# Perceiver block on one core: loads of the first stage on one queue, the first K summed chunk by chunk, first queries turned between the quarters of V

## The chip, the cores and the metric

The kernel runs on one core of a Trainium2 chip. The metric is the device time of one execution in microseconds (us), from the runs of the kernel; beside it there is the profile of one execution. A core has a matrix engine (PE, with its weight loads shown as PEld), a vector engine (DVE), a scalar engine (ACT), GpSimd (POOL) and a sync engine (SP) that only issues transfers. ACT and POOL can issue transfers too. On-chip memory holds the tiles (128 partitions); PE writes into eight accumulation banks, from which ACT or DVE copy.

## What is computed

Thirty-two batches of 64 tokens, 512 features each, attend to 512 context rows of 384 features (16 heads of 32); then the tokens attend to each other, causally and with rotary positions; then half of the tokens of each batch, chosen by a router score, go through a feed-forward layer. All in float32. The first of the three blocks is the one that matters here:

```python
def _L0_xattn_ref(x, context, context_mask, Wq, Wk, Wv, Wo):
    q = (x @ Wq).reshape(B, N, HEADS, hd).transpose(0, 2, 1, 3)
    k = (context @ Wk).reshape(B, M, HEADS, hd).transpose(0, 2, 1, 3)
    v = (context @ Wv).reshape(B, M, HEADS, hd).transpose(0, 2, 1, 3)
    scores = jnp.einsum('bhid,bhjd->bhij', q, k) * scale
    scores = jnp.where(context_mask[:, None, None, :], scores, max_neg)
    attn = jax.nn.softmax(scores, axis=-1)
    out = jnp.einsum('bhij,bhjd->bhid', attn, v)
    return out.transpose(0, 2, 1, 3).reshape(B, N, DIM) @ Wo

x = x + _L0_xattn_ref(_layernorm(x), ctx_768, mask, Wq, Wk, Wv, Wo)
x = x + _L0_attn_ref(_layernorm(x), wq, wk, wv, wo)
x = x + _L0_ffn_ref(_layernorm(x), w_router, W1, b1, W2, b2)
```

## The kernel before

The 2048 token rows are sixteen tiles of 128 rows (`xs[t]`, two batches each); four tiles are a query group (`GT = 4`, eight batches). Every stage is unrolled in Python. A float32 product of 128x128 by 128x512 is two PE instructions, so K of one batch (four pieces of 128 columns, each a sum over three chunks of the context's 384 features) is 24 instructions, and V likewise.

**First stage.** The constants (identity for the transposes, the exponent -0.5, masks) and all sixteen tiles of x are loaded from ACT's queue (lines 74 and 80). The weights of the cross attention, `wk`, `wv`, `wq`, `wo`, are loaded from POOL's queue (164 to 168, through `load`, line 70), each in one transfer; the context of a batch (768 KB, transposed on the host) and its mask come from SP's queue (`load_ctx`, 157). Then, at line 351 and on, PE does K of batch 0 piece by piece (`kv_piece`, 181: three chunks summed into one bank, then a copy, by ACT for K, by DVE for V), V of batch 0, the turns of the first four normalised tiles, and the first group's queries (`query_chunk`, 215). A turn (`query_turn`, 211) is four transposes on PE into bank "pt" and one copy by ACT; `query_norm` (205) writes its rows into a tile `xn` of which there is one. So norm, transposes and copy of one tile alternate. The statistics of a tile (`ln_stats`, 86) are two instructions on DVE and two on POOL. In this stage only PE's order is the written one (`manual_schedule(engines={PE})`); for the other engines a planner orders the instructions.

**Banks.** `bank` (61) names them: "mm" has two, "pt", "po" and "sc0" to "sc3" one each. A product into a bank that is still being copied waits for the copy.

**Loop over batches** (`step`, two steps a batch, all engines in the written order). A step makes the scores of eight heads into sc0 to sc3 (`score_burst`), the softmax on DVE, ACT and POOL into tiles `pr` (a ring of eight), splits and turns the probabilities by transfers on SP's queue (`part`, line 281), joins them one step later (`join`), and uses them two steps later (`attend`). Between them PE works on the next batch's K (first step) or V (second step), and in the first four batches of a group on the next group's turns. At the first step of batch b SP issues the context of batch b + 2.

After the loop come the self attention (lines 509 to 671) and the feed-forward, in which PE's order is written out and the planner orders the rest.

Of the kernel before, what the change touches and what calls it, by code (L numbers as in the profile page):

```python
# [7 lines left out]
F32 = mybir.dt.float32  # L8
U8 = mybir.dt.uint8
# [6 lines left out]
P = 128  # L16
NB, S, D = 32, 64, 512
M, DC = 512, 384
# [4 lines left out]
NC = D // P  # L23
# [19 lines left out]
def perceiver_block(  # L43
# [17 lines left out]
    def bank(tag, shape, name):  # L61
        return psum.tile(shape, F32, tag=tag, name=name, bufs=2 if tag == "mm" else 1)
# [4 lines left out]
    def load(pool, w, tag, name, engine):  # L67
        k, f = w.shape
        t = pool.tile([P, w.shape[0] // P if tag == "W2" else NC, f], F32, tag=tag, name=name)
        engine.dma_start(t[:, : k // P, :], chunked(w))  # L70
        return t

    cst = const.tile([P, C_END], F32, tag="cst", name="cst")
    nc.scalar.dma_start(cst, consts)
    ident = cst[:, C_ID : C_ID + P]

    xs = []
    for t in range(NT):
        xt = xpool.tile([P, D], F32, tag=f"x{t}", name=f"x{t}")
        nc.scalar.dma_start(xt, x[t * P : (t + 1) * P, :])  # L80
        xs.append(xt)

    mv = [const.tile([P, NT, 2], F32, tag=f"mv{n}", name=f"mv{n}") for n in range(3)]
    rstd = [const.tile([P, NT], F32, tag=f"rstd{n}", name=f"rstd{n}") for n in range(3)]
# [11 lines left out]
    def ln_apply(dst, n, t):  # L96
        nc.vector.tensor_scalar(
            dst, xs[t], mv[n][:, t, 0:1], rstd[n][:, t : t + 1], ALU.subtract, ALU.mult
        )

    def transposed(tag, src, name):

        ps = bank(tag, [P, NC, P], f"{name}_tp")
        for c in range(NC):
            nc.tensor.transpose(ps[:, c, :], src[:, c * P : (c + 1) * P], ident)  # L105
        return ps
# [45 lines left out]
    with ExitStack() as pa:  # L152
# [4 lines left out]
        def load_ctx(b):  # L157
            t = kvp.tile([P, NCC, M], F32, tag="ctxT", name=f"ctxT{b}")
            nc.sync.dma_start(t, chunked(ctxT[b]))
            m8 = kvp.tile([P, M], U8, tag="m8", name=f"m8_{b}")  # L160
            nc.sync.dma_start(m8, mask[b : b + 1, :].to_broadcast([P, M]))
            return t, m8

        wk = load(wbpool, xWk, "wk", "xWk", nc.gpsimd)
        ctx0 = load_ctx(0)
        wv = load(wbpool, xWv, "wv", "xWv", nc.gpsimd)
        wq = load(wbpool, xWq, "wq", "xWq", nc.gpsimd)
        wo = load(wbpool, xWo, "wo", "xWo", nc.gpsimd)

        def kv_start(b, loaded):  # L170
            cT, m8 = loaded
            v = kvp.tile([P, NKC, D], F32, tag="v", name=f"v{b}")
            return dict(b=b, cT=cT, m8=m8, kT=[None] * NC, v=v)
# [31 lines left out]
        def query_norm(group, j):  # L205
            g = group["g"]
            xn = wk2.tile([P, D], F32, tag="xn", name=f"xn_a{g}_{j}", bufs=1)
            ln_apply(xn, 0, g * GT + j)
            group["xn"][j] = xn

        def query_turn(group, j):
            ps = transposed("pt", group["xn"][j], f"xn_a{group['g']}_{j}")
            nc.scalar.copy(group["xnT"][:, :, j * P : (j + 1) * P], ps)

        def query_chunk(group, c):
# [131 lines left out]
                return wk2.tile([P, NC, P], F32, tag="oT", name=f"oT_a{half['id']}", bufs=1)  # L347
            return oT

        with tc.manual_schedule(engines={PE}):  # L350
            kv = kv_start(0, ctx0)
            kv_mask(kv)
            for what, i in PIECES:
                kv_piece(kv, what, i)
            group = query_group(0)
            for j in range(GT):
                ln_stats(0, j)
            for j in range(GT):
                query_norm(group, j)
                query_turn(group, j)  # L360
            for c in range(NC):
                query_chunk(group, c)
            nxt = kv_start(1, load_ctx(1))
            kv_mask(nxt)

        with tc.manual_schedule(engines=ALL):
            oT, coming, loaded = None, None, None
            halves = {}

            def step(s):  # L370

                nonlocal kv, nxt, loaded, group, coming, oT
                b, cp = s // 2, s % 2
                g, at = divmod(b, 2 * GT)
                if s and cp == 0:
                    kv = nxt
                    nxt = kv_start(b + 1, loaded) if b + 1 < NB else None
                if cp == 0 and b + 2 < NB:  # L380
                    loaded = load_ctx(b + 2)
                if at == 0 and cp == 0:
                    if g:
                        group = coming
                    coming = query_group(g + 1) if g + 1 < NT // GT else None
                pss = score_burst(kv, group["qT"], cp)
                done, prev = halves.pop(s - 2, None), halves.get(s - 1)
                if done:
                    oT = heads(done, oT)
                    attend(done, oT)  # L390
                half = dict(
                    id=f"{b}_{cp}", kv=kv, cp=cp, last=b == NB - 1, prs=[], tps=[], pTs=[None] * 4
                )
                halves[s] = half
                softmax(half, pss, lambda: join(prev, 0))
                y = None
                for r in range(4):
                    if y is not None and r == 2:
                        residual(*y)
                    if nxt is not None:  # L400
                        kv_piece(nxt, *PIECES[4 * cp + r])
                    else:
                        fill(4 * cp + r)
                    if r == 0:
                        if done and done["cp"]:
                            gather(done, oT)
                        join(prev, 1)
                        join(prev, 2)
                    if r == 1:
                        join(prev, 3)  # L410
                    part(half, r)
                    if r == 1 and done and done["cp"] and done["kv"]["b"] % 2:
                        t = done["kv"]["b"] // 2
                        y = project(oT, t), t
                    if coming is not None:
                        if at < GT:
                            if (cp, r) == (0, 0):
                                ln_stats(0, (g + 1) * GT + at)
                            if (cp, r) == (0, 2):
                                query_norm(coming, at)  # L420
                            if (cp, r) == (1, 0):
                                query_turn(coming, at)
                        if at == 2 * GT - 1 and r % 2:
                            query_chunk(coming, 2 * cp + r // 2)
                if s > 1 and cp and nxt is not None:
                    kv_mask(nxt)
                if s == 2 * NB - 4:
                    norm(0)
                    norm(1)
                    aw["q"] = load(wbpool, aWq, "wq", "aWq", nc.sync)  # L430
                if s == 2 * NB - 3:
                    aw["k"] = load(wbpool, aWk, "wk", "aWk", nc.sync)
                    aw["v"] = load(wbpool, aWv, "wv", "aWv", nc.sync)

            def fill(i):

                before = halves[2 * NB - 2]
                if i == 0:
                    turn(0)
                    qkv(0, "q")  # L440
                elif i == 1:
                    qkv(0, "k")
                elif i == 2:
                    turn(1)
                    norm(2)
                    qkv(0, "v")
                elif i == 3:
                    qkv(1, "q")
                elif i == 4:
                    flip(before, 0, "pt")  # L450
                    qkv(1, "k")
                elif i == 5:
                    flip(before, 1, "pt")
                    qkv(1, "v")
                elif i == 6:
                    flip(before, 2, "pt")
                    turn(2)
                else:
                    flip(before, 3, "pt")
                    qkv(2, "q")  # L460

            for s in range(2 * NB):
                step(s)
            first, second = halves[2 * NB - 2], halves[2 * NB - 1]
            oT = heads(first, oT)
            attend(first, oT)
            qkv(2, "k")
            for r in range(4):
                flip(second, r, f"sc{r}")
            qkv(2, "v")  # L470
            attend(second, oT)
            gather(second, oT)
            residual(project(oT, NT - 1), NT - 1)
            aw["o"] = load(wbpool, aWo, "wo", "aWo", nc.sync)
# [308 lines left out]
```

## Time and profile before

| what | us |
|---|---|
| median of three runs | 1524.06 (1523.72 to 1525.96) |
| the profiled execution's own time | 1528.53 |
| its span, first to last instruction | 1526.5 |
| first instruction of K of batch 0 on PE | 12.10 |
| first instruction of V of batch 0 | 32.69 |
| first turn | 43.45 |
| first query product | 49.54 |
| first scores, begin of the loop's work | 65.71 |
| end of the loop, begin of the self attention | about 945 |
| begin of the feed-forward | about 1330 |

The mean granted clock of PE is 0.993 of full speed. In the first 30 us the transfers move 9.90 MB. A table of waits names the waiting engine and line, what released it, the total in us, how often, and the longest. A timeline line is start, length, engine, line, operation and count, with the idle time before it in brackets. The chain of waits goes back from the last instruction of a stretch to what released each step.

### The profile page before, as it was taken

What the parts mean: (1) busy time and instruction counts of PE and PEld (TensorE: products, weight loads), DVE (VectorE), ACT (ScalarE), POOL (GpSimd) and SP (SyncE); (2) the same over time, 40 slices, a digit from 0 to 9 for tenths busy, and PEclk for the clock granted to TensorE, in tenths of its full rate; (3) what the DMA queues carried; (4) which work ended last, traced back from release to release, by engine and by line L of the source; (5) the groups of instructions that cost most, each with busy time, mean ns of one, the idle gap of its engine ahead of it and who ended that gap; (6) DMA issues with size and microseconds to landing.
All of it is one profiled execution on the core that took longest, in us unless ns stands there. A gap on an engine that the chain in (4) does not pass through costs nothing.

```text
span 1526.5 us, 26359 instructions
## 1 busy us (share of the span) xinstructions
PE 1477.8 (97%) x10592; PEld 690.6 (45%) x10592; DVE 872.0 (57%) x1904; ACT 535.8 (35%) x1049; POOL 679.7 (45%) x504
## 2 busy tenths in 40 slices
PE   5999999999999999999999998999999999999998
PEld 2444444444444444444444443444555555444443
DVE  1377766577766577766576666357776676301001
ACT  0154544344534344534344534222222234300100
POOL 1166655465656465666455656333433432100000
PEclk9999999999999999999999999999999999999999
DMA  7155555345555355545455656010000001411201
GB/s 259 38 105 115 106 117 113 76 95 119 107 107 116 83 91 106 123 100 120 80 91 116 118 103 151 5 56 1 2 2 1 1 2 36 146 40 62 76 0 55
DMA packets 294345, 123.68 MB, mean 81 GB/s; under 512 B 264272, under 2 KB 268368, under 8 KB 294224
## 3 DMA queue, kind: packets, MB, share of 16 engines
q1 hardware_dynamic: 290816, 113.82, 34.9%
q10 hardware_dynamic: 2448, 4.52, 0.8%
q0 software_dynamic: 960, 3.67, 0.6%
q8 instruction: 83, 1.36, 0.4%
q14 instruction: 38, 0.31, 0.1%
HBM read 52.77 MB, written 4.19 MB: 37 GB/s over the span
## 4 chain that ended last, share of the span: by engine, by line
PE 95%; DMA 2%; ACT 1%; DVE 1%; issue 0%; POOL 0%; ACTq 0%; SPq 0%; DVEq 0%
PE kv_v L190 22%; PE kv_k L190 22%; PE hps L500 7%; PE ups L684 7%; PE sc L235 4%; PE po L315 4%; PE q_a L218 4%; PE k_b L141 4%; PE v_b L141 4%; PE y_a L324 4%; PE y_b L589 4%; PE q_b L141 3%; DMA x<-in_x 2%; PE p_b_tp L105 1%; PE po_b L576 1%; PE sc_b L529 1%
## 5 line engine op out<-in xcount | busy, mean ns | idle before, releaser
L261 POOL TENSOR_SCALAR pr<-pr,ri 128x512 f32<-128x512 f32 x256 | 501.8, 1975 | 360.3 <-DVE ri L260 360.3
L190 PE MATMUL kv_k<-ctxT,xWk 128*128 128x512 f32 x768 | 343.7, 603 | 17.2 <-DMA xWk<-in_xWk 12.1
L190 PE MATMUL kv_v<-xWv,ctxT 128*128 128x512 f32 x768 | 343.4, 597 | 0.0
L253 ACT ACTIVATE pr<-pr,mn 128x512 f32<-128x512 f32 x256 | 181.8, 712 | 373.1 <-DVE mn L248 373.1
L190 PEld LDWEIGHTS kv_k<-ctxT,xWk 128*128 128x128 f32 x768 | 144.8, 192 | 192.0 <-issue 163.7
L279 DVE COPY parts<-pr 128x1024 uint16<-128x1024 uint16 x248 | 199.3, 810 | 50.1 <-POOL pr L261 50.1
L190 PEld LDWEIGHTS kv_v<-xWv,ctxT 128*128 128x128 f32 x768 | 142.7, 190 | 167.5 <-issue 155.3
L248 DVE CUSTOM_DVE_ANT_0 pr<-sc,mb 128x512 f32<-128x512 f32 x256 | 165.3, 684 | 26.4 <-PE sc L235 25.7
L292 ACT COPY pT<-tp 128x1024 uint16<-128x1024 uint16 x124 | 142.4, 1165 | 0.0
L196 DVE COPY v<-kv_v 128x512 f32<-128x512 f32 x128 | 87.4, 682 | 94.7 <-PE kv_v L190 94.7
L193 ACT COPY kT<-kv_k 128x512 f32<-128x512 f32 x128 | 74.8, 586 | 135.2 <-PE kv_k L190 135.2
L294 DVE COPY pT<-tp 128x1024 uint16<-128x1024 uint16 x124 | 120.3, 973 | 0.0
L500 PE MATMUL hps<-selT,w 128*128 128x512 f32 x256 | 114.6, 601 | 0.0
L684 PE MATMUL ups<-W,hT 128*128 128x512 f32 x256 | 111.3, 594 | 0.0
L689 DVE TENSOR_TENSOR up<-ups,b_bc 128x512 f32<-128x512 f32 x8 | 5.5, 692 | 166.9 <-PE ups L684 166.9
L315 PEld LDWEIGHTS po<-pT,v 128*32 128x32 f32 x4096 | 60.1, 110 | 51.8 <-issue 42.1
L684 PEld LDWEIGHTS ups<-W,hT 128*128 128x128 f32 x256 | 48.3, 190 | 62.3 <-issue 62.3
L500 PEld LDWEIGHTS hps<-selT,w 128*128 128x128 f32 x256 | 48.3, 193 | 57.0 <-issue 57.0
L235 PE MATMUL sc<-kT,qT_a 32*64 32x512 f32 x1024 | 71.3, 613 | 0.0
L315 PE MATMUL po<-pT,v 128*32 128x64 f32 x4096 | 70.4, 220 | 0.0
L91 POOL TENSOR_SCALAR ve<-mv 128x1 f32<-128x1 f32 x48 | 10.6, 220 | 131.9 <-DVE mv L89 131.9
L504 ACT ACTIVATE hT<-hps,b_sb 128x512 f32<-128x512 f32 x32 | 22.0, 687 | 134.5 <-PE hps L500 134.5
(102 smaller groups left out, 1464.6 us busy)
## 6 DMA issues: line engine op xcount, KB each, us to landing
ctxT<-in_ctxT SPq DMA_DIRECT2D x32, 768.0 KB, 4.9
w<-in_W SPq DMA_DIRECT2D x32, 256.0 KB, 2.7
x<-in_x ACTq DMA_DIRECT2D x16, 256.0 KB, 9.8
W<-in_W SPq DMA_DIRECT2D x1, 4096.0 KB, 14.5
out<-o SPq DMA_DIRECT2D x16, 256.0 KB, 2.0
tp<-parts SPq DMA_TRANSPOSE x248, 3.2
m<-in_mask SPq DMA_DIRECT2D x32, 64.0 KB, 4.5
xWq<-in_xWq POOLq DMA_DIRECT2D x1, 1024.0 KB, 17.5
```

The costliest lines, as they stand in the source:

```text
L141: nc.tensor.matmul(ps, tok[t]["xnT"][:, d, :], w[:, d, :], start=(d == 0), stop=(d == NC - 1))
L190: nc.tensor.matmul(ps, lhsT, rhs, start=(d == 0), stop=(d == NCC - 1))
L235: nc.tensor.matmul(pss[r][S * i : S * (i + 1), :], qT[2 * cp + i][rows, at : at + S], kv["kT"][2 * cp + i][rows, :], start=True, stop=True,)
L248: nc.vector.tensor_tensor_reduce(out=pr, in0=pss[r], in1=kv["mb"], scale=1.0, scalar=3.4e38, op0=ALU.add, op1=ALU.min, accum_out=mn,)
L253: nc.scalar.activation(pr, pr, AF.Exp, bias=mn, scale=-1.0, accum_out=su)
L261: nc.gpsimd.tensor_scalar(pr, pr, ri, None, ALU.mult)
L279: nc.vector.tensor_copy(parts, pr.bitcast(U16).rearrange("p (k e) -> p e k", e=2))
L292: nc.scalar.copy(dst, src)
L294: nc.vector.tensor_copy(dst, src)
L315: nc.tensor.matmul(po[32 * r : 32 * r + 32, c, :], v[:, k, HD * h : HD * (h + 1)], half["pTs"][r][:, k, S * i : S * (i + 1)], start=(k == ...
L500: nc.tensor.matmul(ps, w1[:, d, :], selT[n][:, d, :], start=(d == 0), stop=(d == NC - 1))
L684: nc.tensor.matmul(ps, hTs[n][fc][:, j * P : (j + 1) * P], w2[:, fc, :], start=(fc == 0), stop=(fc == NFC - 1),)
```

## The change

All loads of the first stage are issued by SP, in the order in which they are used: wk and the first context alternately in three chunks each of 128 rows (256 KB), the first mask, the constants, x0 to x3, wv, wq, the second context with its mask, x4 to x7, wo. The tiles x8 to x15 are issued by SP in the loop, one at the first step of each of the first eight batches, ahead of that step's context load.

K of batch 0 is summed over the chunks in the outer loop: four pieces stand in four banks (two "mm", "pt", "po") and each chunk adds to all four; then ACT copies the four.

The first four tiles are normalised at once into four tiles of the ring `pr`, and their turns are put between V's pieces: V0, V1, turn 0, V2, turn 1, V3, turn 2, turn 3, into sc0 to sc3. In this stage all engines follow the written order. The number of PE instructions is the same.

```diff
-    nc.scalar.dma_start(cst, consts)
-    xs = []
-    for t in range(NT):
-        xt = xpool.tile([P, D], F32, tag=f"x{t}", name=f"x{t}")
-        nc.scalar.dma_start(xt, x[t * P : (t + 1) * P, :])
-        xs.append(xt)
+    xs = [xpool.tile([P, D], F32, tag=f"x{t}", name=f"x{t}") for t in range(NT)]
+    def load_x(t):
+        nc.sync.dma_start(xs[t], x[t * P : (t + 1) * P, :])
...
-        wk = load(wbpool, xWk, "wk", "xWk", nc.gpsimd)
-        ctx0 = load_ctx(0)
-        wv = load(wbpool, xWv, "wv", "xWv", nc.gpsimd)
-        wq = load(wbpool, xWq, "wq", "xWq", nc.gpsimd)
-        wo = load(wbpool, xWo, "wo", "xWo", nc.gpsimd)
+        wk = wbpool.tile([P, NC, D], F32, tag="wk", name="xWk")
+        cT0 = kvp.tile([P, NCC, M], F32, tag="ctxT", name="ctxT0")
+        for d in range(NCC):
+            nc.sync.dma_start(wk[:, d, :], xWk[d * P : (d + 1) * P, :])
+            nc.sync.dma_start(cT0[:, d, :], ctxT[0, d * P : (d + 1) * P, :])
+        m80 = kvp.tile([P, M], U8, tag="m8", name="m8_0")
+        nc.sync.dma_start(m80, mask[0:1, :].to_broadcast([P, M]))
+        nc.sync.dma_start(cst, consts)
+        for t in range(GT):
+            load_x(t)
+        wv = load(wbpool, xWv, "wv", "xWv", nc.sync)
+        wq = load(wbpool, xWq, "wq", "xWq", nc.sync)
+        ctx1 = load_ctx(1)
+        for t in range(GT, 2 * GT):
+            load_x(t)
+        wo = load(wbpool, xWo, "wo", "xWo", nc.sync)
...
-        def query_turn(group, j):
-            ps = transposed("pt", group["xn"][j], f"xn_a{group['g']}_{j}")
+        def query_turn(group, j, tag="pt"):
+            ps = transposed(tag, group["xn"][j], f"xn_a{group['g']}_{j}")
...
-        with tc.manual_schedule(engines={PE}):
-            kv = kv_start(0, ctx0)
+        with tc.manual_schedule(engines=ALL):
+            kv = kv_start(0, (cT0, m80))
             kv_mask(kv)
-            for what, i in PIECES:
-                kv_piece(kv, what, i)
+            pss = [bank(tag, [P, M], f"kv0_k{i}") for i, tag in enumerate(("mm", "mm", "pt", "po"))]
+            for d in range(NCC):
+                for i in range(NC):
+                    nc.tensor.matmul(
+                        pss[i], wk[:, d, i * P : (i + 1) * P], kv["cT"][:, d, :],
+                        start=(d == 0), stop=(d == NCC - 1),
+                    )
+            for i in range(NC):
+                kT = kvp.tile([P, M], F32, tag=f"kT{i}", name=f"kT0_{i}", bufs=1 + i // 2)
+                nc.scalar.copy(kT, pss[i])
+                kv["kT"][i] = kT
             group = query_group(0)
             for j in range(GT):
                 ln_stats(0, j)
             for j in range(GT):
-                query_norm(group, j)
-                query_turn(group, j)
+                xn = sm3.tile([P, D], F32, tag="pr", name=f"xn_a0_{j}", bufs=8)
+                ln_apply(xn, 0, j)
+                group["xn"][j] = xn
+            for i in range(NKC):
+                kv_piece(kv, "v", i)
+                if i:
+                    query_turn(group, i - 1, f"sc{i - 1}")
+            query_turn(group, GT - 1, f"sc{GT - 1}")
             for c in range(NC):
                 query_chunk(group, c)
-            nxt = kv_start(1, load_ctx(1))
+            nxt = kv_start(1, ctx1)
             kv_mask(nxt)
...
+                if cp == 0 and 2 * GT + b < NT:
+                    load_x(2 * GT + b)
                 if cp == 0 and b + 2 < NB:
                     loaded = load_ctx(b + 2)
```

## The prediction, made before the changed kernel was run

> **What bounds the kernel now.** I read the page first, then the waits of PE alone, then the chain of waits in the first 60 us, then PE's timeline there, then windows of one microsecond for transfer rate and granted clock. The page: PE is busy for nearly the whole span, so only PE's time counts. At its foot are the transfers' times to landing.
>
> ```profile
> PE 1477.8 (97%) x10592; PEld 690.6 (45%) x10592; DVE 872.0 (57%) x1904; ACT 535.8 (35%) x1049; POOL 679.7 (45%) x504
> ...
> w<-in_W SPq DMA_DIRECT2D x32, 256.0 KB, 2.7
> x<-in_x ACTq DMA_DIRECT2D x16, 256.0 KB, 9.8
> W<-in_W SPq DMA_DIRECT2D x1, 4096.0 KB, 14.5
> ...
> cst<-in_consts ACTq DMA_DIRECT2D x1, 321.5 KB, 4.5
> ```
>
> Where does PE wait? From 66 to 945 us (the loop over batches) its list of waits is empty. In the first 60 us (what waited, for what, total us, times, longest):
>
> ```profile
> PE kv_k L190 <- DMA xWk<-in_xWk: 12.1, 1, 12.1
> PE kv_k L190 <- ACT kT L193: 5.1, 1, 5.1
> PE xn_a_tp L105 <- DVE xn_a L97: 2.5, 3, 0.9
> PE q_a L218 <- ACT xnT_a L213: 0.7, 1, 0.7
> ```
>
> The chain of waits says why the 5.1 us exist: ACT's sequencer issues the sixteen loads of x and is held at them until 25.47, so its first copy of K is late and PE has no free bank.
>
> ```profile
> 25.47 1.28 ACT L193
> ...
> 27.41 5.49 PE kv_k L190 x6
> 32.89 10.73 PE kv_v L190 x24
> ```
>
> PE's timeline gives the end of this stage (start, length, line, work, count): four turns with gaps, 32 query instructions, and the first scores at 65.71. Behind these PE never waits in the loop, so what counts is how much earlier 65.71 becomes.
>
> ```profile
> 43.45 0.60 PE L105 MATMUL xn_a_tp<-cst,xn_a 128*128 128x128 f32 x4
> ...
> 47.78 1.09 PE L105 MATMUL xn_a_tp<-cst,xn_a 128*128 128x128 f32 x4 [0.79 <-DVE xn_a L97]
> 49.54 16.24 PE L218 MATMUL q_a<-xnT_a,xWq 128*128 128x512 f32 x32 [0.67 <-ACT xnT_a L213]
> 65.71 1.11 PE L235 MATMUL sc<-kT,qT_a 32*64 32x512 f32 x16
> ```
>
> The loop shows the same work warm: a turn between V's pieces takes 81.41 - 80.97 = 0.44 us, and V without it 89.23 - 78.29 - 0.44 = 10.50 us for 24 instructions, 0.4375 each.
>
> ```profile
> 78.29 2.84 PE L190 MATMUL kv_v<-xWv,ctxT 128*128 128x512 f32 x6
> 80.97 0.60 PE L105 MATMUL xn_a_tp<-cst,xn_a 128*128 128x128 f32 x4
> 81.41 7.89 PE L190 MATMUL kv_v<-xWv,ctxT 128*128 128x512 f32 x18
> 89.23 1.11 PE L235 MATMUL sc<-kT,qT_a 32*64 32x512 f32 x16
> ```
>
> The windows give rate and clock (last three columns: granted clock, DMA share, GB/s). xWo, issued at 3.81, lands after 20.8 us, so from 25 on only the 256 KB pieces of x on ACT's queue move: 387 to 391 GB/s from one queue. After its 5.1 us pause PE has clock 0.50: one instruction per 0.853 us (weight loads start at 28.42, 29.27, 30.13), 0.425 more than warm (34.44, 34.87).
>
> ```profile
> 25.00:26.00 1.00, 0.00 (x0) 0.00 (x0) 0.00 (x0) 0.53 (x1) 0.00 (x0) 1.00 1.06 389
> 26.00:27.00 1.00, 0.00 (x0) 0.00 (x0) 0.00 (x0) 0.99 (x2) 0.00 (x0) 0.89 1.05 387
> 28.00:29.00 1.00, 1.00 (x2) 0.34 (x1) 0.00 (x0) 0.33 (x1) 0.00 (x0) 0.50 1.06 391
> ```
>
> **The stage as it is**: 12.10 start, 20.59 K (10.50 warm, 5.13 pause, the rest half clock), 10.76 V, 6.09 turns with waits, 16.17 queries; sum 65.71.
>
> **The start.** wk and the first context come as three pairs of 256 KB pieces at the head of SP's queue instead of 768 KB at once among 9.9 MB. Bounds: a 256 KB w lands 2.7 us after issue, so two issues (0.74 + 0.45) give 3.9 as the floor; the whole first context (768 KB, sharing the engines) took 6.1 us, 6.8, as the ceiling. I take 5.2, where cst, issued at 0.73 and nearest in size to a pair, landed (0.73 + 4.5). Gain 6.9 us.
>
> **K by chunks.** 24 instructions as before, 10.50 warm. The three starts after a pause ran at half speed for 5 (from 12.10), 7 (from 27.41) and 5 (from 49.54) instructions; 6 x 0.425 = 2.55, so 13.05, K ends at 18.25. A pair's 8 instructions need at least 3.4 us; the pair needs 512 KB / 387 GB/s = 1.36 us, so the second and third are there in time. ACT issues nothing now. If its table load (1.28) came only behind the first finished bank: that bank is done 6 instructions (2.6 us) before the end, and 1.28 + 0.59 fit. V's first piece waits for nothing; without this cover it would cost 1.3. Gain 20.59 - 13.05 = 7.54.
>
> **Is wv there?** Ahead of it and with it go 768 + 768 + 64 + 321.5 + 1024 + 768 = 3713.5 KB, 3.80 MB: 9.8 us at 387 GB/s. The trace's packets of the first context begin at 3.0, 2.3 after its issue, and end at 6.0, 0.9 before its landing at 6.8; so wv lands at 3.0 + 9.8 + 0.9 = 13.7, against 18.25: 4.5 us of cover, gone below 3.80 MB / 14.35 us = 265 GB/s. W's 4096 KB in 14.5 us from issue is 289 already with its latency. wq lands 2.7 us later, needed at 31. SP's 21 issues (0.45 each, 9.5 us) run ahead of the data.
>
> **The normalised rows.** x3 lands near 11.7; statistics 0.69 + 0.18 on DVE, 0.23 + 0.53 on POOL, four applies of 0.55: ready by 15.5. The first turn stands behind two pieces of V, at 23.5: covered by 8 us. DVE now has V's copies queued behind the applies by hand; they are needed only from 20.9 on. POOL begins with the mask of batch 0 and then the powers; the mask lies ahead of cst in the queue, so that wait delays nothing. POOL also loses four issues (3.3 us), all off the path.
>
> **V and turns.** V 10.50 (before 10.76). Four turns at 0.44 and one last wait for ACT 0.67: 2.43 for 6.09. The turns go to sc0 to sc3, so none waits for the copy of the one before. Gain 0.26 + 3.66.
>
> **Queries.** PE stays warm: 32 x 0.4375 = 14.0, before 16.17. Gain 2.1.
>
> **The loop.** Eight loads of x move to SP, ahead of a context load and the transposes. An issue there can take 1.20 to 1.95 us (ctxT at 91.99 and 117.58), a transfer 0.7. They are for rows used four batches later or more. In 66 to 945 us no engine's waits name a transfer, so I take 0; uncovered, up to 8 x (1.95 + 0.7) = 21. A gain is excluded: PE waits for nothing there. The four pr buffers lent to the first rows are free after the last turn, before the first softmax. After 945 us DVE, ACT and POOL are ordered by the planner, which may choose anew; PE's gaps from 945 to 1330 us sum to 385 - 363.8 = 21. I take 0, with 3 either way.
>
> **Sum.** 5.2 + 13.05 + 10.50 + 2.43 + 14.0 = 45.2 for 65.7: 20.5 us. The profiled execution (1528.53, span 1526.5, 2.0 around it) becomes 1508.0, span 1506.0. It lies 4.5 above the median of the runs, 1524.06, which becomes **1503.6**.
>
> **Rivals.**
> 1. *K stays at half clock.* If chunk gaps keep PE from warming through all 24 instructions, K costs 24 x 0.425 = 10.2 extra instead of 2.55: 7.7 lost, 1511.3. Against: a cold pair takes 6.8 us, the next pair 1.4. The Trainium skill ("TensorE: Matmul & The Clock Gate", Part 1) says that a free-running window of about 3.4 us has to be busy first; here the half clock after 27.41 lasted 6.1 us. By the page K has 4 to 8 cold instructions, 12.2 to 13.9.
> 2. *Transfers bound V moderately.* At the worst single 1 MB row (aWq, 6.8 us, 154 GB/s), wv lands at 24.7 + 3.9 = 28.6, and PE, cold again for 5 instructions (2.1), ends the stage 29.1 later, at 57.7: 8.0 gained, 1516.
> 3. *Slower: one queue hands its pieces on slowly.* From 9 to 17 us the pieces of x landed every 2.8 us, 94 GB/s. If that were the queue's own pace, wv would land at 40.4 + 3.9 = 44.3 and the first scores start at 73.4: 7.7 later, 1531.8. It decides from wv landing after 36.6, a pace under 116 GB/s. For: the row itself, three queues' worth of pieces now on one. Against: alone on its queue x ran at 387. The Trainium skill ("DMA: Bandwidth & Descriptors", Rules for kernel authors and Anatomy of one DMA) speaks against this change: at least 1 MiB per DMA, and about 2.0 us plus bytes / 436e3 for each. An estimate from that page, if nothing overlapped, lands wv at 35.4: 1522.9. The 387 GB/s of 256 KB pieces contradict the serial reading.
> 4. *Given back.* The eight x loads or the planner's new order cost PE what the start gained: 1524. Against: the empty list of waits.
>
> **How the numbers follow.** Forecast 0.84, half clock 0.04, moderate 0.05, slower 0.03, given back 0.04. The forecast's own range: start 3.9 to 6.8, K 12.6 to 13.5 by 5 to 7 cold instructions, the planner 3 either way: 1499 to 1508. Reaching over the half-clock case, 1499 to 1512. A measurement of this kernel tells about 0.2%, 3 us, from no change. Faster 0.93 (cases 1 and 2 are faster too); same 0.03; slower 0.04.
>
> **What would show it.** PE's first kv_k near 5.2 and no pause before kv_v near 18; no wait for ACT's kT; wv landed before V; turns of 0.44 between V's pieces; clock 1.00 through the queries; first scores near 45; the loop's waits still empty; 945 to 1330 as long as before. A kv_v waiting for xWv, cold K to its end, or waits for tp in the loop would make me wrong.

## The result, and the profile after

The changed kernel takes 1504.44 us, the median of five runs (1503.81 to 1509.14), beside 1524.06 for the kernel before (five runs, 1523.16 to 1527.44): a ratio of 0.9875 with a 95% interval of 0.9861 to 0.9889, 19.6 us less. Forecast were 1503.6, in a range of 1499 to 1512. The profiled execution took 1508.6 us, its span is 1506.6.

The page after: PE's busy time is nearly what it was (1477.8), its share of the span is up; POOL issues four transfers less.

```profile
PE 1474.5 (98%) x10592; PEld 689.9 (46%) x10592; DVE 871.4 (58%) x1904; ACT 535.7 (36%) x1049; POOL 676.8 (45%) x500
```

PE's waits of the first 60 us, in the form of the list shown of before (what waited, for what, total us, times, longest). The waits for ACT's copy of K and for the normalised rows are gone; the wait for the first transfers fell from 12.1 to 4.2.

```profile
PE kv_k L366 <- DMA ctxT<-in_ctxT: 4.2, 1, 4.2
PE q_a L228 <- ACT xnT_a L223: 0.7, 1, 0.7
```

PE's timeline of the changed kernel (start, length, line, work, count). The stage runs without a gap but the one before the queries, and the first scores come at 44.13 instead of 65.71.

```profile
4.21 13.22 PE L366 MATMUL kv_k<-ctxT,xWk 128*128 128x512 f32 x24 [4.21 <-DMA ctxT<-in_ctxT]
17.26 5.31 PE L200 MATMUL kv_v<-xWv,ctxT 128*128 128x512 f32 x12
...
28.44 1.04 PE L102 MATMUL xn_a_tp<-cst,xn_a 128*128 128x128 f32 x8
30.20 14.00 PE L228 MATMUL q_a<-xnT_a,xWq 128*128 128x512 f32 x32 [0.73 <-ACT xnT_a L223]
44.13 1.11 PE L245 MATMUL sc<-kT,qT_a 32*64 32x512 f32 x16
```

Step by step, in us (the lengths are differences of these starts; the self attention begins at the first turn of its first tile, 943.19 before and 921.61 after; its end and the last product are read from the same timeline):

| step | before | forecast | after |
|---|---|---|---|
| first K instruction | 12.10 | 5.2 | 4.21 |
| K of batch 0 | 20.59 | 13.05 | 13.05 |
| V, turns, last wait | 16.85 | 12.93 | 12.94 |
| queries | 16.17 | 14.0 | 13.93 |
| first scores at | 65.71 | 45.2 | 44.13 |
| loop | 877.48 | as before | 877.48 |
| self attention with its fillers, to the last product `row` | 387.21 | as before, 3 either way | 388.66 |
| from there to the last product's start | 189.25 | as before | 189.58 |

So in this pair of profiles 21.6 us were gained at the start, and 1.8 of them are missing at the end: 1.45 in the self attention, 0.33 behind it, where a product waits for a tile `w` that lands at 1318.37. Where the 1.45 went is seen at the end of the loop, here in PE's timeline of the kernel before and then of the one after: a turn, the pause until ACT has copied it, then queries, keys and the second turn.

```profile
943.19 0.66 PE L105 MATMUL xn_b_tp<-cst,xn_b 128*128 128x128 f32 x4
946.66 3.70 PE L141 MATMUL q_b<-aWq,xnT_b 128*128 128x512 f32 x8 [2.82 <-ACT xnT_b L134]
951.56 3.67 PE L141 MATMUL k_b<-aWk,xnT_b 128*128 128x512 f32 x8 [1.19 <-DMA aWk<-in_aWk]
955.07 0.60 PE L105 MATMUL xn_b_tp<-cst,xn_b 128*128 128x128 f32 x4
```

```profile
921.61 0.66 PE L102 MATMUL xn_b_tp<-cst,xn_b 128*128 128x128 f32 x4
925.08 6.72 PE L138 MATMUL q_b<-aWq,xnT_b 128*128 128x512 f32 x8 [2.82 <-ACT xnT_b L131]
931.65 3.60 PE L138 MATMUL k_b<-aWk,xnT_b 128*128 128x512 f32 x8
935.08 0.60 PE L102 MATMUL xn_b_tp<-cst,xn_b 128*128 128x128 f32 x4
```

The pause of 2.82 was there before. After the change the eight query instructions behind it take 6.72 instead of 3.70, and the wait of 1.19 for aWk is gone, since aWk lands while they crawl: turn to turn 13.47 instead of 11.88. Windows of the changed kernel show the granted clock at 0.50 there. (A window line is the stretch, its length, the busy time and count of PE, PEld, DVE, ACT and POOL, the granted clock, the busy share of the transfers' engines and GB/s.)

```profile
920.96:924.37 3.41, 1.30 (x56) 0.97 (x44) 3.03 (x12) 2.74 (x7) 1.43 (x1) 1.00 0.74 82
924.37:927.78 3.41, 2.70 (x3) 1.18 (x4) 0.75 (x2) 2.78 (x5) 3.41 (x3) 0.50 0.76 237
```

The five runs of the changed kernel are of two kinds: mean clock 0.999 and 1503.8 to 1504.4 us in three, 0.996 and 1508.6 to 1509.1 in two. The profiled one is of the second kind. Its clock is at half twice behind the loop: for 6.83 us from 924.37 on, and for 3.41 us from 1238.40 on. The profile of the kernel before has only the second of these (3.41 us from 1258.98 on). A kernel below with x loaded at once has neither in its profile, at mean clock 0.999, and its self attention takes 385.22: 1.97 less than the changed kernel's up to the second turn and 1.47 less behind it. So the table holds for the two profiled runs. Which steps make up the difference of the medians was not recorded.

### The profile page after: what moved, and what is told of

Read it like the earlier page. It is cut to its first block, busy times and chain, and to the rows that moved or that the text cites. A ratio compares the mean times of both kernels' runs of the same rounds, so it can differ in the third digit from the quotient of the medians.

```text
span 1506.6 us, 26366 instructions
## 1 busy us (share of the span) xinstructions
PE 1474.5 (98%) x10592; PEld 689.9 (46%) x10592; DVE 871.4 (58%) x1904; ACT 535.7 (36%) x1049; POOL 676.8 (45%) x500
## 4 chain that ended last, share of the span: by engine, by line
PE 96%; ACT 1%; DMA 1%; DVE 1%; issue 0%; POOL 0%; ACTq 0%; SPq 0%; DVEq 0%
PE kv_v L200 22%; PE kv_k L200 22%; PE ups L711 7%; PE hps L527 7%; PE sc L245 4%; PE po L325 4%; PE q_b L138 4%; PE k_b L138 4%; PE q_a L228 4%; PE v_b L138 4%; PE y_a L334 4%; PE y_b L616 4%; PE p_b_tp L102 1%; PE kv_k L366 1%; PE po_b L603 1%; PE sc_b L556 1%
## 5 line engine op out<-in xcount | busy, mean ns | idle before, releaser
L200 PE MATMUL kv_k<-ctxT,xWk 128*128 128x512 f32 x744 | 328.1, 596 | 0.0
L200 PEld LDWEIGHTS kv_k<-ctxT,xWk 128*128 128x128 f32 x744 | 138.8, 190 | 166.7 <-issue 156.2
```

The source lines that it names most:

```text
L200: nc.tensor.matmul(ps, lhsT, rhs, start=(d == 0), stop=(d == NCC - 1))
```

## The experiments

Each starts from the changed kernel. "First scores" is the start of the first sc product on PE in the profile of that run (44.13 in the changed kernel), the quantity that all the steps act on; the times scatter by the clock as just seen. The experiments ran on three chips, on which the kernel before took 1526.51 (the first four), 1523.72 (the next four) and 1523.41 us (the last two). So times of different chips are compared by their ratio to the kernel before, which is 0.9875 for the changed kernel.

**The loads as before, PE's order as after.**

```diff
-            nc.sync.dma_start(wk[:, d, :], xWk[d * P : (d + 1) * P, :])
-            nc.sync.dma_start(cT0[:, d, :], ctxT[0, d * P : (d + 1) * P, :])
...
+        nc.scalar.dma_start(cst, consts)
+        for t in range(NT):
+            nc.scalar.dma_start(xs[t], x[t * P : (t + 1) * P, :])
+        wk = load(wbpool, xWk, "wk", "xWk", nc.gpsimd)
+        cT0, m80 = load_ctx(0)
...
-                if cp == 0 and 2 * GT + b < NT:
-                    load_x(2 * GT + b)
```

> PE's new order with the loads of before (constants and all sixteen x on ACT's queue, the weights on POOL's, x not loaded in the loop). Theory (queues and PE order each give a part): PE starts at 12.1 when wk lands, K takes 13.1, ACT is held at its x issues until 25.5 and its first copy (table load 1.28 and copy 0.59) lets V start at 27.4, then 12.9 for V with turns and 13.9 for queries: first scores at 54, 10 later than in the changed kernel, about 1514.5 us. Rival (the PE order alone does it): first scores near 45, about 1504.5. Rival (the queues alone do it): first scores near 65, about 1524.

First scores at 54.14, 1516.42 us (1515.33 to 1517.65), ratio 0.9936 (0.9921 to 0.9950). Its waits of PE in the first 80 us:

```profile
PE kv_k L359 <- DMA xWk<-in_xWk: 12.0, 1, 12.0
PE kv_v L193 <- ACT kT L365: 3.1, 1, 3.1
```

The loads' queues, order and pieces together are worth 10.0 us of the 21.6: 7.75 by the start (11.96 for 4.21), 3.1 by ACT's copies held behind its sixteen issues, less 1.0 because K's clock was full earlier in this run (12.07 for 24 instructions). PE's order gives the rest. Both rivals, the one that gave all to the queues and the one that gave all to PE, are out. What each of the three things done to the loads is worth alone was not run; a kernel with wk and the first context whole at the head of SP's queue is missing.

**K summed piece by piece.**

```diff
-            for d in range(NCC):
-                for i in range(NC):
-                    nc.tensor.matmul(
-                        pss[i], wk[:, d, i * P : (i + 1) * P], kv["cT"][:, d, :],
-                        start=(d == 0), stop=(d == NCC - 1),
-                    )
             for i in range(NC):
...
+                kv_piece(kv, "k", i)
```

> The changed kernel with K of batch 0 summed piece by piece again. Theory (summing by chunks only hides the landing of the second and third pair): the first piece starts near 4.2 and waits until the third pair has landed near 7.3; 20 instructions remain; first scores at 45.5 to 46, 1.5 to 2 later than in the changed kernel, 1505 to 1507 us. Rival (the chunks are what makes the early start): K begins only near 7.3 and costs 13, first scores at 47, and with a clock at half for longer 48 to 50, 1508 or more.

First scores at 44.66, only 0.5 later, 1508.12 us (1504.82 to 1509.26), ratio 0.9874 as the changed kernel's. I had expected 1.5 to 2, so this is a miss. PE's weight loads show the waits (start, length, in brackets the idle time before):

```profile
4.30 0.50 PEld L200 LDWEIGHTS kv_k<-ctxT,xWk 128*128 128x128 f32 x2 [4.30 <-DMA xWk<-in_xWk]
6.40 0.50 PEld L200 LDWEIGHTS kv_k<-ctxT,xWk 128*128 128x128 f32 x2 [1.60 <-DMA xWk<-in_xWk]
7.74 0.29 PEld L200 LDWEIGHTS kv_k<-ctxT,xWk 128*128 128x128 f32 x1 [0.84 <-DMA xWk<-in_xWk]
```

The first piece does wait for the second pair, but the clock was at half until 10.1, and two instructions at half clock take 1.7 us. The pairs came 2.1 and 1.3 us apart, so PE stood for some 0.4 us before the second and not at all before the third. K took 13.46 instead of 13.05. So with the first pair at the head of the queue in pieces, the sum over four banks adds little: those 0.4.

**The turns behind V again, one row tile.**

```diff
-            for j in range(GT):
-                xn = sm3.tile([P, D], F32, tag="pr", name=f"xn_a0_{j}", bufs=8)
-                ln_apply(xn, 0, j)
-                group["xn"][j] = xn
             for i in range(NKC):
                 kv_piece(kv, "v", i)
-                if i:
-                    query_turn(group, i - 1, f"sc{i - 1}")
-            query_turn(group, GT - 1, f"sc{GT - 1}")
+            for j in range(GT):
+                query_norm(group, j)
+                query_turn(group, j)
```

> The changed kernel with the four turns behind V again, one row tile, one bank. Theory: the turns with their waits take 6.1 instead of 2.4 and PE falls to half clock for 5 query instructions (2.1): first scores at 50, 5.8 later, about 1510 us. Rival (the turns cost only their waits, the clock stays): first scores at 47.8, about 1508. Rival (the turns were hidden anyway): 44, about 1504.5.

First scores at 51.03, 6.9 later, 1512.50 us (1511.37 to 1513.92), ratio 0.9910 (0.9895 to 0.9925). V to queries took 17.76 (16.94 to 34.70) instead of 12.94 and the queries 16.33 instead of 13.93: the turns cost their waits and the clock, as the theory says. The 1.1 beyond it is in the main a wait of the first turn (1.24) for a row that, in the written order, DVE normalises only behind V's copies.

**All of x at once, none in the loop.**

```diff
+        for t in range(2 * GT, NT):
+            load_x(t)
...
-                if cp == 0 and 2 * GT + b < NT:
-                    load_x(2 * GT + b)
```

> The changed kernel with x8 to x15 issued at once behind wo, none in the loop. Theory (the loads in the loop cost nothing): first scores at 44, the loop takes as long as before to 0.1 us, time the same as the changed kernel within 1 us apart from the clock. Rival (the loop's loads cost PE): the loop from first scores to the self attention gets shorter by up to some us.

First scores at 43.66, the self attention at 921.14: the loop takes 877.48 as in both kernels. The loads in the loop cost nothing. 1505.05 us (1503.92 to 1505.55), ratio 0.9860 (0.9845 to 0.9874); in its profiled run the clock stays full at the end of the loop, and turn to turn takes 11.50, with a span of 1502.6.

**The first mask later.**

```diff
-        m80 = kvp.tile([P, M], U8, tag="m8", name="m8_0")
-        nc.sync.dma_start(m80, mask[0:1, :].to_broadcast([P, M]))
         nc.sync.dma_start(cst, consts)
...
         wq = load(wbpool, xWq, "wq", "xWq", nc.sync)
+        m80 = kvp.tile([P, M], U8, tag="m8", name="m8_0")
+        nc.sync.dma_start(m80, mask[0:1, :].to_broadcast([P, M]))
...
-            kv_mask(kv)
...
+            kv_mask(kv)
             nxt = kv_start(1, ctx1)
```

> The changed kernel with the first mask's load behind wq instead of behind the first context, and its use on POOL behind the queries. Theory (the 64 KB mask, 128 packets of 512 B, holds up the one queue from 7 to 9.5 us): the dip in the transfer rate leaves 6 to 9 us, x0 to x3 and wv land about 2.5 us earlier (wv near 13.7 instead of 16.3); first scores do not move (44 to 44.5), since V is bound by K's end. Rival (the dip is the wait of SP's issues for earlier loads): the dip stays at 6 to 9 us.

Windows of the changed kernel, then of this one; the last column, GB/s, is the one to read. (The clock's column says 1.00 ahead of the first change on record, which is at 9.60 in the changed kernel. That K begins at half clock is read from PE's weight loads: they start at 7.75, 8.61 and 9.46, then at 9.96, 10.39 and 10.82.)

```profile
7.00:8.00 1.00, 1.00 (x3) 0.48 (x2) 0.00 (x0) 0.00 (x0) 0.00 (x0) 1.00 0.31 50
8.00:9.00 1.00, 1.00 (x2) 0.42 (x2) 0.00 (x0) 0.00 (x0) 0.00 (x0) 1.00 0.21 53
10.00:12.00 2.00, 2.00 (x6) 0.91 (x5) 0.00 (x0) 0.00 (x0) 0.62 (x1) 1.00 1.04 402
```

```profile
7.00:8.00 1.00, 1.00 (x3) 0.48 (x2) 0.00 (x0) 0.00 (x0) 0.00 (x0) 1.00 0.99 320
8.00:9.00 1.00, 1.00 (x3) 0.48 (x2) 0.00 (x0) 0.00 (x0) 0.00 (x0) 1.00 0.98 375
```

The dip goes with the mask. x0 is used from 9.62 on instead of 12.26, and wv, issued at 6.02 with 7.6 to landing, is there at 13.6 instead of 16.3 (7.99 + 8.3). First scores at 44.34 as expected: V waits for K. One run, 1505.96 us.

**Two queues for the first pieces.**

```diff
-            nc.sync.dma_start(cT0[:, d, :], ctxT[0, d * P : (d + 1) * P, :])
+            nc.scalar.dma_start(cT0[:, d, :], ctxT[0, d * P : (d + 1) * P, :])
```

(and the first mask likewise)

> The changed kernel with the three pieces of the first context and its mask issued by ACT, the rest by SP. Theory (one queue costs only its issue times): first piece pair lands 0.45 earlier, PE starts near 3.8 instead of 4.2, and because the clock needs its busy window first, first scores gain 0.2 to 0.5: 43.7. Rival (one queue is slower than two for this data): pairs two and three land over 1 us earlier, wv too, PE's start under 3.5.

PE starts at 4.23, not earlier: issued at the same moment, the first pieces take 3.3 and 3.5 us to land instead of 2.7 and 2.9 one after the other. My 3.8 was wrong, and so is the rival's start under 3.5. One part of the rival did come true: wv, issued at 7.23 with 6.9 to landing, is there at 14.1 instead of 16.3. Whether that is the second queue or the mask, which no longer lies ahead of it in SP's queue, this run does not separate; PE waits for wv in neither kernel. First scores at 43.02, but that is the clock, full from 7.3 in this run and from 9.6 in the changed kernel's. One run, 1503.48 us.

**Products ahead of the first K.**

```diff
+            ones = sm3.tile([P, M], F32, tag="pr", name="ones", bufs=8)
+            nc.vector.memset(ones, 1.0)
+            warm = bank("sc0", [P, M], "warm")
+            for n in range(2):
+                nc.tensor.matmul(warm, ones[:, 0:P], ones, start=True, stop=True)
```

> The changed kernel with two additional products of a tile of ones into sc0 ahead of the first K (4 instructions that no output uses). Theory (K's 13.05 are 10.3 plus the half clock of PE's first 3.4 to 6.8 us): the clock becomes full some 3 us earlier, K takes 11 to 12, first scores 42.5 to 43.5, 1 to 1.5 earlier; time 1503 or so, within the scatter of the clock. Rival (the clock doesn't count these, or they delay the first K): first scores at 44 or later.

```profile
1.44 3.78 PE L365 MATMUL warm<-ones 128*128 128x512 f32 x4 [1.44 <-DVE ones L362]
5.01 10.51 PE L371 MATMUL kv_k<-ctxT,xWk 128*128 128x512 f32 x24
```

K takes 10.35 and is done 1.9 earlier although it starts 0.8 later; first scores at 42.24. The half clock at K is worth 2.70 here, for the 2.55 of the forecast. The time did not follow: 1506.08 us (1503.63 to 1506.68), ratio 0.9883 (0.9868 to 0.9897). The profiled run (1503.63) has half clock at the end of the loop for 3.4 us (eight queries in 5.40); the other three runs have a lower mean clock, 0.997 for 0.998, and where they lost it was not recorded.

**The pause at the end of the loop.** The first turn of the self attention goes between V's pieces of batch 31, and two weight loads ahead of transposes.

```diff
+                    if s == 2 * NB - 3 and r == 3:
+                        aw["v"] = load(wbpool, aWv, "wv", "aWv", nc.sync)
                     part(half, r)
...
+                    if s == 2 * NB - 3 and r == 0:
+                        turn(0)
...
                     aw["q"] = load(wbpool, aWq, "wq", "aWq", nc.sync)
-                if s == 2 * NB - 3:
                     aw["k"] = load(wbpool, aWk, "wk", "aWk", nc.sync)
-                    aw["v"] = load(wbpool, aWv, "wv", "aWv", nc.sync)
...
-                    turn(0)
                     qkv(0, "q")
```

> The changed kernel with the first turn of the self attention moved into the last but one step before the loop's end (between V pieces of batch 31) and the loads of its K and V weights issued one step and one transpose earlier. Theory (the gap of 2.8 us at the end of the loop costs itself, and half clock for 7 us where the clock's window catches it): no gap there, the stretch from the last context products to the second turn shrinks from 13.5 (half clock) or 11.5 to 12 (full) to 8 or 9; time 1500 to 1502 with less scatter between runs. Rival (the gap only moves to the next wait, such as the weights' landing or the banks): the stretch stays above 11, time as the changed kernel's.

```profile
922.13 3.70 PE L138 MATMUL q_b<-aWq,xnT_b 128*128 128x512 f32 x8
925.66 3.60 PE L138 MATMUL k_b<-aWk,xnT_b 128*128 128x512 f32 x8
929.10 0.60 PE L102 MATMUL xn_b_tp<-cst,xn_b 128*128 128x128 f32 x4
```

No pause, no wait, 6.97 to the second turn, and 0.44 for the turn moved. 1500.48 us (1499.83 to 1500.94), ratio 0.9847 (0.9831 to 0.9864): 4.0 below the changed kernel's median, taken on another chip. At full clock the stretch is shorter by 11.50 - 7.41 = 4.1, which agrees, and all four runs lie within 1.1 us. The turn and the two loads were moved together; what each gives alone was not run.

**The three together, and the changed kernel once more on the same chip.** Early turn, late mask, and products of 512 and 256 columns.

> The changed kernel with three of the edits together: the early turn and weight loads at the end of the loop, the first mask behind wq, and products of ones ahead of the first K (512 and 256 columns; no output uses them). Theory (the two gains add, since both shorten what PE does in a row): first scores at 42, no gap at the end of the loop, about 2 below the kernel with the early turn alone, 1498 to 1499 us. Rival (the clock takes the gain back at another place): 1500 or more, with a half-clock stretch somewhere after the loop.

> The changed kernel itself once more, on the same chip as the kernel with three edits. Theory: 1504 where the clock stays full at the end of the loop, up to 1509 where its window catches the gap there; the difference of its runs follows their mean clock.

The changed kernel again: 1504.53 us, ratio 0.9868 (0.9852 to 0.9885), with 1508.74 at mean clock 0.996 and 1503.95 to 1504.86 at 0.999, as expected. The three together: 1500.63 us (1499.46 to 1501.09), ratio 0.9843 (0.9828 to 0.9857), no better than the early turn alone. In the profiled run (1499.46) the first scores come at 42.90, 1.3 before those of the early turn alone (44.21), and the span is 1.6 shorter; K begins at half clock here, in spite of the products ahead of it, and takes 11.74. The other runs (1500.4 to 1501.1) don't show the gain. The expected sum is not shown by the times.

## Why the prediction was right

- **The start.** Forecast 5.2, measured 4.21. I had taken the landing of cst, which shared its time with x and the weights; the row of the lone 256 KB load, kept as the floor (3.9), was the nearer one. This is the largest single error of the sum, 1.0.
- **K by chunks.** 13.05 was met, but not because of the chunks: they save some 0.4. The gain of 7.54 is ACT's release (5.13 of pause) and one half-clock stretch less. That the half clock makes 2.7 of K is shown by the products ahead of it. The exact hit is luck: in the seven profiles in which K is summed like this from about 4.2 to 4.4 on, with no products ahead of it, it takes 11.92 to 13.17, as the clock becomes full at another point of K in each. The forecast's 12.6 to 13.5 was too narrow for that.
- **wv in time.** Right in effect, wrong in size: 16.3 instead of 13.7, a cover of about 1 us instead of 4.5. The step "3.80 MB at 387 GB/s" left out that the mask's 64 KB move far below that rate; with the mask behind wq, wv landed at 13.6. The trace of before had shown it: the first context landed at 6.8, and POOL's wait for the mask issued behind it ended at 9.60. The rows were later for the same reason (x0 used from 12.26 on, where the forecast had x3 land at 11.7), which the 8 us of cover hid.
- **Turns and queries.** 12.94 and 13.93 for 12.93 and 14.0; undone, they cost 6.9.
- **The loop.** Zero, shown by 877.48 in the kernels before and after and in the one without these loads.
- **After the loop.** I had feared the planner; the waits of PE there are the same lines with the same sums, but for aWk's that is gone. The 1.45 are in the main the granted clock behind the first pause (1.59 from turn to turn). The forecast's 3 either way held it, for a wrong reason.
- **The rivals.** Transfers bounding V, and the slower case of pieces handed on at 94 GB/s, fell: from 10 to 12 us one queue moved 256 KB pieces at 402 GB/s. So the rule of the Trainium skill ("DMA: Bandwidth & Descriptors", Rules for kernel authors) of at least 1 MiB per DMA does not bind where pieces follow each other in one queue. The estimate of 35.4 for wv took the sum that the Trainium skill ("DMA: Bandwidth & Descriptors", Anatomy of one DMA) gives for loads issued by GpSimd, and these are SP's; wv landed at 16.3. K at half clock throughout fell, too: the clock was full from 9.6 on. And nothing was given back in the loop. Two slips changed no result: rival 2 took aWq's 6.8 us as the worst 1 MB row, and aWv's is 8.2, which by the same sum makes some 1521 for 1516; and the chances of "same" and "slower" stand the other way round than the cases (given back 0.04, slower 0.03).

Two errors of opposite sign, 1.0 at the start and 1.8 behind it, nearly cancel in the profiled run: 1508.6 for the forecast 1508.0. From there the forecast took off the 4.5 us by which the profiled run of the kernel before lay above its median. That the changed kernel's profiled run lies as far above its own (4.2) is luck, since three of its five runs are of the other kind. So the mechanism of the start is shown, while the closeness of the median, 1504.44 for 1503.6, is in part chance.

## What to carry to other kernels

Before the first product, order the loads by use; the first operands were cut here as well, and what the cut alone is worth is open. Look also at which engine's queue must issue them, since an engine held at its issues is late with its copies. A pause of PE should be priced twice, once as idle time and once as the half clock that may follow, and the second depends on when it falls. A gain at the start reaches the end only if the pauses behind it stay as they were: in the profiled run the next one took 1.6 us of it, and closing it gave some 4 us more. A transfer should be priced by its own row and not by its bytes: the mask's 64 KB cost wv 2.7 us.

## What the runs showed of the hardware

**When a pause costs clock.** The half-clock stretches inside these executions last 3.41 or 6.83 us. The Trainium skill ("TensorE: Matmul & The Clock Gate", Part 1) speaks of a free-running window of about 3.4 us; the traces agree: in the changed kernel the clock changes at 9.60, 924.37, 931.20, 1238.40 and 1241.81, and these lie 268, 2, 90 and 1 times 3.413 us apart, the length of the shortest stretch. The same pause of 2.82 us left PE 1.30 of 3.41 us busy in the changed kernel's window (38%, shown above), and the clock halved. In the kernel with the loads as before it fell across two windows, with 73% and 44%, and the clock stayed:

```profile
929.78:933.19 3.41, 2.49 (x84) 1.36 (x68) 3.41 (x10) 1.55 (x5) 0.25 (x1) 1.00 0.97 110
933.19:936.60 3.41, 1.51 (x4) 0.79 (x5) 1.55 (x6) 3.41 (x7) 3.41 (x3) 1.00 0.58 141
```

So in these runs a pause shorter than a window halved the clock or not by its place alone. The busy share does not decide it alone, though. The changed kernel's clock halves once more behind a window in which PE was busy for 63%:

```profile
1234.98:1238.40 3.42, 2.17 (x79) 1.80 (x76) 3.35 (x8) 0.91 (x3) 1.77 (x1) 1.00 0.02 5
1238.40:1241.81 3.41, 3.41 (x49) 1.74 (x34) 3.41 (x7) 1.28 (x3) 0.00 (x0) 0.50 0.00 0
```

That window holds only small products, of 128 columns and less. In the kernel with x loaded at once a window at the same place of the work (from 1233.81 on) is busy for 63% as well but ends with products of 512 columns, and the clock stays. What the clock goes by beside the busy time is not shown.

**A mask of 64 KB.** Read once for each of 128 partitions in packets of 512 B, it cut the one queue to 50 GB/s for two microseconds (7 to 9) while everything behind it waited; behind wq it made no such dip. Each is seen in one profile, and in that of the kernel before the mask landed 2.7 us after the context issued ahead of it.
